# Four dense tiles instead of two in a graph-attention kernel, with the list work moved earlier

## The chip, the cores and the metric

The kernel runs on one core of one Trainium2 chip. The core has five engines with a queue each, worked off in order: PE (matrix products), DVE (vector work), ACT (activations and copies), POOL (here almost only the issue of indirect DMAs, that is gathers and scatters by a list of row numbers) and SP (the issue of plain DMAs). They meet at semaphores only. The metric is the device time of one execution in microseconds (us); less is better.

## The reference

Two layers on a graph of 4096 nodes with 128 features each. `adj` is a 4096 x 4096 matrix of 0 and 1 with about 66 ones in a row.

```python
# layer 0: attention with 8 heads over the neighbours, then a projection and a layer norm
Wh = einsum('nd,hde->hne', nodes, W); f1 = Wh . a1; f2 = Wh . a2
e = leaky_relu(f1[:, :, None] + f2[:, None, :], 0.2)
att = softmax(where(adj > 0, e, -9e15), axis=-1)
h = elu(einsum('hnm,hmd->hnd', att, Wh))
x = layernorm(nodes + elu(cat(h) @ W1 + b1)) * gamma + beta
# layer 1: of a node's neighbours every skip-th is dropped; then quantiles over the rest
svals = sort(where(keep[:, :, None], x[None, :, :], big), axis=1)   # feature by feature
agg = mean of svals at ceil(0.25 n), ceil(0.5 n), ceil(0.75 n)
out = (0.5 * agg + 0.5 * x) @ W.T + b + x
```

Both layers need, for each node, the list of its neighbours.

## The kernel before

A **tile** is 128 nodes. There are 32 tiles in six **blocks** (`BLOCKS`: 2, then five times 6); inside a block the nodes are sorted by their number of neighbours. The first layer (`gat`, from L936) runs as one long program in which four kinds of work are interleaved; the second (`sparse`, from L2180) follows it.

**The front** (`Front`, from L315) makes the neighbour lists from `adj`, in *pieces* (`pieces`, L866). For a tile: `scan` packs the row's bits into words with matmuls, `first` draws the largest words off with `max`. For a block: `second` in four parts, `place`, which scatters the block's lists to a DRAM table `rows_d` by indirect DMAs on POOL (L651), and `keep`, which stores them once more for the second layer. After the last block, `close` sets the order for the second layer. There are 69 pieces that count; 57 are left when the main loop starts.

**The list tiles** take two **half tiles** each (64 nodes; the loop index `u`). `load(u)` gathers the neighbours' features by indirect DMAs on POOL, one DMA for each slot of 128 rows (L1141), some 34 in a half tile, into a ring of six buffers, which is three half tiles. `probabilities(u)` forms the softmax of them on DVE and ACT (e at L1226), `rows_sum(u)` spreads it over columns (DVE, L1274) and sums with matmuls (PE, L1282); `collect` copies the sums, and after four half tiles `combine` takes two tiles through W, elu, W1, the layer norm (DVE up to L1367) and two scatters to `x1_d` on POOL (L1370). The loop over `u` (from L1616) emits in each turn: rows_sum(u), some pieces of the front (`advance`), probabilities(u + 1), a step of the dense tiles, load(u + 3), collect and a step of each running `combine`, and more steps of the dense tiles.

**The dense tiles** (`full`, from L1382) are the last `FULLS = 2` tiles, with the most neighbours. Their attention is made from whole rows of `adj`, without gathers of neighbours. A **unit** is one head over half a row: SP loads two 128x1024 pieces of f2 (L1457), DVE adds the mask and takes the maximum (L1468), ACT adds f1 (L1489), DVE makes the leaky relu (L1491), ACT the exponential (L1497), PE transposes 16 blocks (L1511) that ACT copies (L1516), and PE sums against x (L1523). 32 units in all. `full` is a generator: two steps to set up, one a unit, six for its `combine`. For a new tile the four quarters of the mask are fetched from `adj` by indirect DMAs on POOL (L1439) into one buffer, and turned into bf16 by DVE (L1447); the next quarter is fetched after that. x is held for this in the buffer `soon`, which is used for gathers of the second layer later.

The steps are taken when the front is done (`todo` empty): one after probabilities, one after `combine`, and one more in every second half tile, 2.5 a half tile.

**The hand-over**: near the end of the loop the dense steps are run out, and 24 gathers for the second layer's first tile (into `soon`, L1668) are issued on POOL after the last gather of the lists; then follow the last scatters to `x1_d` and the second layer, which sorts rows on DVE (L2254) with copies on ACT (L2247), its rows gathered by POOL (L2209).

A scheduler sets the final order of instructions on each engine from what is emitted; waits are semaphores.

Of the kernel before, what the change touches and what calls it, by code (L numbers as in the profile page):

```python
# [38 lines left out]
F32 = mybir.dt.float32  # L39
# [11 lines left out]
P = 128  # L51
N = 4096
D = 128
NT = N // P
H = 8
# [19 lines left out]
MERGE = 128  # L75
# [6 lines left out]
XF = D + 2 * H  # L82
# [20 lines left out]
BLOCKS = (2, 6, 6, 6, 6, 6)  # L103
# [3 lines left out]
DONE = START[-1] * P  # L107
SHARED = (("rowdata", ROW, I32), ("work", MERGE, F32), ("mask_s", C1, I32), ("k3", C3, F32))

FULLS = 2  # L110
LISTED = NT - FULLS
ROWS = 18
SPREAD = 9
TWO = 2
# [821 lines left out]
def gat(  # L936
# [28 lines left out]
    with ExitStack() as ctx:  # L965
# [131 lines left out]
        def own_row(t):  # L1097
            indices(t)
            if t % TWO == 0:
                if t < LISTED:  # L1100
                    me = tp.tile([P, TWO, XF], F32, name="me", bufs=5)
                else:
                    me = front.one.tile([P, max(BLOCKS), MERGE], F32, name="ids_a")
                    me = me.rearrange("p t c -> p (t c)")[:, : TWO * XF]
                    me = me.rearrange("p (j d) -> p j d", d=XF)
# [196 lines left out]
        def combine(t, zT, pair):  # L1302
# [66 lines left out]
            for j in range(TWO):  # L1369
                done = nc.gpsimd.indirect_dma_start(  # L1370
                    out=x1_d,
                    out_offset=bass.IndirectOffsetOnAxis(ap=index[t + j][3][:, 0:1], axis=0),
                    in_=s[:, j, :],
                    in_offset=None,
                )
                for other in stored:
                    tc.declare_no_dep(done.ins, other, reason="each node has a row of its own")
                for other in ahead:
                    tc.declare_no_dep(done.ins, other, reason="rows of earlier blocks alone")
                stored.append(done.ins)  # L1380

        def full():  # L1382

# [37 lines left out]
            ]  # L1421
            buffers = nzs + [a_is[:2]]
            units = [(j, h, q) for j in range(FULLS) for h in range(H) for q in range(2)]
            own_row(LISTED)
            own_row(LISTED + 1)
            rows = tp.tile([P, FULLS, 4], I32, name="rows_f", bufs=1)
            for j in range(FULLS):
                for q in range(4):
# [32 lines left out]
            def best(n):  # L1461
# [5 lines left out]
                for i, v in enumerate(buffers[n % 3]):  # L1467
# [10 lines left out]
                f1 = mes[LISTED + j][:, j, D + H + h : D + H + h + 1]  # L1478
# [52 lines left out]
            def close(j, h):  # L1531
# [19 lines left out]
                def turn():  # L1551
                    ps = fr.psum_w.tile([P, 2, NG1], F32, name="ps_words")
                    ps = ps.rearrange("p m c -> p (m c)")[:, :P]
                    nc.tensor.transpose(ps, z[:, :P], c["idf"])
                    nc.scalar.copy(zT[h][:, ts(j, P)], ps)

                return turn

# [8 lines left out]
            best(0)  # L1567
            exps(0)
            yield
            turn, many = None, len(units)  # L1570
            for n in range(many):
                if n + 2 < many:
                    begin(n + 2)
                changing = n + 1 < many and units[n + 1][0] != units[n][0]
                if n + 2 < many and units[n + 2][0] != units[n][0] and not changing:
                    fetch_mask(1, 0, a_is[2])
                if changing:
                    for q in range(4):
                        make_mask(q, a_is[2])
                        if q < 3:  # L1580
                            fetch_mask(1, q + 1, a_is[2])
                if n + 1 < many:
                    best(n + 1)
                pTs = [turned(n, 0), turned(n, 1)]
                if turn is not None:
                    turn()
                    turn = None
                summed(n, 0, pTs[0])
                pTs.append(turned(n, 2))
                summed(n, 1, pTs[1])  # L1590
# [4 lines left out]
                    exps(n + 1)  # L1595
                if units[n][2] == 1:
                    turn = close(*units[n][:2])
                yield
            turn()
            for _ in combine(  # L1600
                LISTED,
                zT.__getitem__,
                lambda h: [(zT[h + i].unsqueeze(1), i, i + 1) for i in range(TWO)],
            ):
                yield

        stored, ahead = [], []
        held = {u: load(u) for u in range(3)}
        advance(EARLY)
        f1s = {0: spread_f1(0)}  # L1610
# [5 lines left out]
        for u in range(halves_of):  # L1616
# [5 lines left out]
            with tc.issue_after(spread):  # L1622
                if u < 2 * START[1]:
                    advance((4, 2, 1, 1)[u])
                elif todo:
                    advance(2 if u in (5, 8) or u > 12 and u % 3 == 0 else 1)
            if u == 1:
                with tc.issue_after(front.scattered):
                    held[3] = load(3)
# [23 lines left out]
            with ExitStack() as after:  # L1653
# [1187 lines left out]
```

## Time and profile before

| | us |
|---|---|
| median of three runs (7160.54 to 7166.68) | 7163.81 |
| the profiled execution's own time | 7162.36 |
| its span, first to last instruction | 7160.6 |
| first gather of the lists starts (L1141) | 84.2 |
| last gather of the lists ends | 2811.1 |
| first gather of the second layer (L2209) | 2858.6 |

Busy in the span: PE 1368.8, DVE 5647.0, ACT 2305.9, POOL 4285.1. These averages mix two stages. In the first, up to about 2860, POOL issues one gather after another and DVE is busy about half of the time; in the second DVE is busy 4190.74 us of the 4260 from 2900 to 7160.

How to read the views: a row of groups gives line, engine, operation, tiles, count, busy time, mean of one, then the idle time of the engine just before these instructions and what ended it. "issue" stands where the engine waited for nothing that the profile shows. A view of stretches gives, for each engine, busy time and number of instructions in a stretch.

### The profile page before, as it was taken

To read this page: it belongs to the slowest core of one execution; us is meant where nothing else is said; L and a number is where in the kernel's file an instruction comes from. 1 tells how busy PE (TensorE), PEld (TensorE's weight loads), DVE (VectorE), ACT (ScalarE), POOL (GpSimd) and SP (SyncE) were. 2 spreads that over 40 slices of the span, in tenths; PEclk is the share of its full clock that TensorE was granted. 3 is DMA by queue.
4 is the path that set the end of the run, shared out by engine and by line. 5 is a ranking of instruction groups with operands and counts; after the bars stand their busy time and mean duration, and the time that the engine had idled before them with its cause. 6 is when DMAs were issued, how large, how long until landed. Compare 5 with 4: busy or idle time off the path is not lost. (4 is left out here: it accounts for less than half of the span.)

```text
span 7160.6 us, 33915 instructions
## 1 busy us (share of the span) xinstructions
PE 1368.8 (19%) x7581; PEld 1097.7 (15%) x7581; DVE 5647.0 (79%) x8486; ACT 2305.9 (32%) x2777; POOL 4285.1 (60%) x4316
## 2 busy tenths in 40 slices
PE   6342443432245563000000000000000000000000
PEld 3232332322235563000000000000000000000000
DVE  6553553544554553899999999999999999999998
ACT  3010111100023342344444434444344344444343
POOL 5777777777777777754656656446355345554500
PEclk6666666666667786555555555555555555555555
DMA  7432433332243332211111111111011111111100
GB/s 236 94 111 58 109 79 88 94 62 63 56 126 106 100 97 54 52 35 33 42 33 36 36 32 44 31 33 43 25 39 41 26 30 38 36 33 29 39 0 2
DMA packets 286970, 415.39 MB, mean 58 GB/s; under 512 B 188611, under 2 KB 189764, under 8 KB 286740
## 3 DMA queue, kind: packets, MB, share of 16 engines
q0 software_dynamic: 140560, 302.48, 17.2%
q1 hardware_dynamic: 146196, 110.66, 5.5%
q14 instruction: 153, 1.25, 0.1%
q8 instruction: 61, 1.00, 0.1%
HBM read 400.05 MB, written 13.17 MB: 58 GB/s over the span
## 5 line engine op out<-in xcount | busy, mean ns | idle before, releaser
L2254 DVE TENSOR_TENSOR rows<-low,rows 128x1024 f32<-128x1024 f32 (+7 forms) x2118 | 3425.8, 1664 | 66.7 <-ACT low L2247 43.0
L2209 POOL DMA_INDIRECT rows<-x_d,info x2054 | 2068.7, 1007 | 1704.5 <-ACT picked L2309 1087.2
L1141 POOL DMA_INDIRECT nb<-xf_d,ids x2035 | 2004.5, 985 | 639.3 <-issue 593.2
L2247 ACT COPY low<-rows 128x1024 f32<-128x1024 f32 (+8 forms) x1059 | 1452.1, 1377 | 2060.8 <-DVE rows L2254 1986.7
L2316 PE MATMUL low<-sixth_i,picked 128*128 128x128 f32 x300 | 72.6, 423 | 3960.8 <-ACT low L2247 3756.2
L1226 DVE TENSOR_TENSOR e<-nb,ps_small 128x64 f32<-128x64 f32 (+9 forms) x185 | 44.2, 241 | 875.8 <-DMA nb<-xf_d,ids 867.4
L2316 PEld LDWEIGHTS low<-sixth_i,picked 128*128 128x128 f32 x300 | 63.7, 316 | 3969.8 <-ACT low L2247 3764.9
L1282 PE MATMUL ps_z<-spread,nb 128*128 128x128 f32 x4180 | 532.1, 293 | 183.4 <-DVE spread L1274 183.3
L1282 PEld LDWEIGHTS ps_z<-spread,nb 128*128 128x128 f32 x4180 | 529.7, 210 | 200.9 <-DVE spread L1274 128.4
L2254 DVE TENSOR_TENSOR rows<-low_s,rows 128x512 f32<-128x512 f32 (+3 forms) x1056 | 531.3, 538 | 2.7 <-ACT low_s L2247 1.9
L1256 ACT ACTIVATE ps_e<-ps_e 128x288 f32<-128x288 f32 (+9 forms) x60 | 23.3, 388 | 1468.1 <-DVE ps_e L1250 1468.1
L1274 DVE TENSOR_TENSOR spread<-e,ps_small 128x1024 f32<-128x1024 f32 (+4 forms) x284 | 313.9, 1129 | 125.0 <-PE ps_z L1282 113.5
L2247 ACT COPY low_s<-rows 128x512 f32<-128x512 f32 (+3 forms) x528 | 247.6, 503 | 307.9 <-DVE rows L2254 230.3
L2356 POOL DMA_INDIRECT out<-o,info x32 | 35.0, 1094 | 383.5 <-ACT o L2352 353.1
L400 PE MATMUL ps_words<-nz,pows 128*128 128x256 bf16 (+1 forms) x544 | 239.7, 612 | 21.1 <-ACT nz L393 11.9
L393 ACT ACTIVATE nz<-a_i 128x1024 bf16<-128x1024 int32 x128 | 134.8, 1055 | 278.1 <-PE ps_words L400 184.4
L1313 PE MATMUL ps_h<-zT,w_ga 128*128 128x256 f32 x240 | 100.9, 579 | 380.0 <-DVE s L1864 328.8
L1523 PE MATMUL ps_small<-soon,lists 128*128 128x128 f32 x768 | 125.9, 322 | 166.9 <-DVE e L1235 66.3
L197 DVE SCALAR_TENSOR_TENSOR key<-key,k 128x256 f32<-128x256 f32 x320 | 148.2, 478 | 1.1
L2258 DVE TENSOR_TENSOR rows<-rows 128x256 f32<-128x256 f32 (+7 forms) x259 | 146.1, 570 | 0.0
L193 DVE MAX8 k<-key 128x8 f32<-128x256 f32 x352 | 141.5, 418 | 1.0
L1523 PEld LDWEIGHTS ps_small<-soon,lists 128*128 128x128 f32 x768 | 115.2, 232 | 174.3 <-DVE e L1235 67.2
(388 smaller groups left out, 2750.5 us busy)
## 6 DMA issues: line engine op xcount, KB each, us to landing
a_i<-in_adj SPq DMA_DIRECT2D x128, 512.0 KB
rows<-x_d,info POOLq DMA_INDIRECT x2054
nb<-xf_d,ids POOLq DMA_INDIRECT x2035
nz<-f_d SPq DMA_DIRECT2D x44, 512.0 KB
a_i<-f_d SPq DMA_DIRECT2D x20, 512.0 KB
xf_d<-xf POOLq DMA_DIRECT2D x4, 576.0 KB
soon<-xf_d SPq DMA_DIRECT2D x32, 72.0 KB
me<-rows_d SPq DMA_DIRECT2D x30, 72.0 KB
```

The source lines that it names most:

```text
L193: nc.vector.max(out=top, in_=work)
L197: nc.vector.scalar_tensor_tensor(work, work, top[:, 7:8], work, op0=ALU.is_lt, op1=ALU.mult)
L400: nc.tensor.matmul(ps_w[:, :m, ts(i, 2 * part)], self.pows[:, b, :], bits[:, :m, :, b], start=b == 0, stop=b == WBITS - 1,)
L1141: gather = nc.gpsimd.indirect_dma_start(out=rows[:, used + i, :], out_offset=None, in_=xf_d, in_offset=bass.IndirectOffsetOnAxis(ap=ids[:, ...
L1274: last = nc.vector.tensor_tensor(spread[:, :m], e[:, at : at + m, :].unsqueeze(2).to_broadcast(shape), own.unsqueeze(1).unsqueeze(3).to_br ...
L1282: product = nc.tensor.matmul(ps_z[:, g, :], rows[:, k, :D], spread[:, i].rearrange("p j h -> p (j h)"), start=i0 + i == 0, stop=i0 + i == ...
L1523: nc.tensor.matmul(fr.small[:, ts(q, P)], pT[:, ts(i, P)], xs[:, m, :] if m < NT * 3 // 4 else later[:, m - NT * 3 // 4, :], start=4 * g + ...
L2209: return nc.gpsimd.indirect_dma_start(out=row, out_offset=None, in_=x1_d, in_offset=bass.IndirectOffsetOnAxis(ap=info[:, col : col + 1], a ...
L2247: nc.scalar.copy(packed, lows)
L2254: done = nc.vector.tensor_tensor(to, packed, highs, op=op)
L2258: nc.vector.tensor_tensor(lows, lows, highs, op=ALU.min)
L2316: product = nc.tensor.matmul(made["ps"], v, to, start=i == 0, stop=i == len(found))
```

## The change

`FULLS` goes from 2 to 4, so there are 28 list tiles (56 half tiles) and four dense ones (64 units). The own rows of the dense tiles share one buffer, the mask is fetched for each next tile, and the dense tiles are combined in two pairs: the first pair's `combine` runs beside the third tile's units. The front gives two pieces a half tile from `u = 8` on (before: one, and two in every third after `u = 12`), so it ends at `u = 29` instead of 41. The dense steps are one more a half tile: 3.5 in the mean. `combine` of the list tiles takes two steps a turn in the last block. The dense steps are run out, and the 24 gathers for the second layer emitted, one half tile nearer to the end; these gathers are declared free of the dense tiles' scatters.

```diff
-FULLS = 2
+FULLS = 4
...
+                    at = t - LISTED
+                    if not at:
+                        me = front.one.tile([P, max(BLOCKS), MERGE], F32, name="ids_a")
+                        me = me.rearrange("p t c -> p (t c)")[:, : FULLS * XF]
+                        mes["full"] = me.rearrange("p (j d) -> p j d", d=XF)
+                    me = mes["full"][:, at : at + TWO, :]
...
+                if t >= LISTED:
+                    last.append(done.ins)
...
-            own_row(LISTED)
-            own_row(LISTED + 1)
+            for j in range(FULLS):
+                own_row(LISTED + j)
...
-                    nc.scalar.copy(zT[h][:, ts(j, P)], ps)
+                    nc.scalar.copy(zT[h][:, ts(j % TWO, P)], ps)
...
+            def finished(j):
+                return combine(
+                    LISTED + j,
+                    zT.__getitem__,
+                    lambda h: [(zT[h + i].unsqueeze(1), i, i + 1) for i in range(TWO)],
+                )
...
-                    fetch_mask(1, 0, a_is[2])
+                    fetch_mask(units[n + 2][0], 0, a_is[2])
...
-                            fetch_mask(1, q + 1, a_is[2])
+                            fetch_mask(units[n + 1][0], q + 1, a_is[2])
...
+                if n and n % (2 * H * TWO) == 0:
+                    steps = finished(n // (2 * H) - TWO)
+                    next(steps)
...
+                if steps is not None:
+                    next(steps, None)
                 yield
...
-                    advance(2 if u in (5, 8) or u > 12 and u % 3 == 0 else 1)
+                    advance(2 if u in (5, 8) or u > 7 else 1)
...
-                for stages in going:
+                for stages in going * (2 if u >= 2 * START[-1] else 1):
                     next(stages, None)
-            if rest is not None:
+            for _ in range(2 if rest is not None else 0):
                 next(rest, None)
-            if u + 3 == halves_of:
+            if u + 2 == halves_of:
                 for _ in rest:
                     pass
...
+                        for other in last:
+                            tc.declare_no_dep(
+                                done.ins, other, reason="rows of earlier blocks alone"
+                            )
```

More of the change, by code (lines that the diff above doesn't have):

```diff
@@ L1102, in own_row @@
                 else:
-                    me = front.one.tile([P, max(BLOCKS), MERGE], F32, name="ids_a")
-                    me = me.rearrange("p t c -> p (t c)")[:, : TWO * XF]
-                    me = me.rearrange("p (j d) -> p j d", d=XF)
+                    at = t - LISTED
[4 more added lines that the diff above has]
+                    me = mes["full"][:, at : at + TWO, :]
                 for j in range(TWO):
@@ L1477, in best @@
                     )
-                f1 = mes[LISTED + j][:, j, D + H + h : D + H + h + 1]
+                f1 = mes[LISTED + j][:, j % TWO, D + H + h : D + H + h + 1]
                 most, less = k[:, 4 * q + 2 : 4 * q + 3], k[:, 8 + q : 9 + q]
@@ L1569, in full @@
             yield
-            turn, many = None, len(units)
+            turn, many, steps = None, len(units), None
+            def finished(j):
[4 more added lines that the diff above has]
+                )
             for n in range(many):
@@ L1597, in full @@
                     turn = close(*units[n][:2])
+                if steps is not None:
+                    next(steps, None)
                 yield
             turn()
[L1600 to L1604, printed above, removed]
+            for _ in finished(FULLS - TWO):
                 yield
-        stored, ahead = [], []
+        stored, ahead, last = [], [], []
         held = {u: load(u) for u in range(3)}
```

## The prediction

> **What bounds the kernel now.** I read first the page's slices: POOL is at 7 tenths in slices 1 to 16 with DVE below it in all but the last, then DVE at 9. So there are two stages, and the change touches the first alone. The built order of the second stage's instructions is the same on all engines, so I take its 4302 us (2858.6 to 7160.6) as fixed and ask when its first gather can start.
>
> What bounds the first stage: the costliest group, and POOL's waits up to the last gather (us in total, times, longest).
>
> ```profile
> L1141 POOL DMA_INDIRECT nb<-xf_d,ids x2035 | 2004.5, 985 | 639.3 <-issue 593.2 <-PE ps_z L1282 14.0 <-DMA nb<-xf_d,ids 11.0
> ```
>
> ```profile
> POOL nb L1141 <- issue: 593.2, 1947, 0.3
> POOL nb L1141 <- PE ps_z L1282: 14.0, 8, 7.3
> POOL nb L1141 <- DMA nb<-xf_d,ids: 11.0, 36, 0.3
> ...
> POOL a_i L1439 <- DVE high L1447: 4.4, 1, 4.4
> ```
>
> The reader is to see that 2004.5 + 593.2 us of the 2727 between first and last gather are issue, each gather behind the last. A busy share of 76% is thus a full queue. Who consumes has slack; DVE's waits from 2080 to 2340 and 2380 to 2700, where the dense units run:
>
> ```profile
> DVE e L1226 <- DMA nb<-xf_d,ids: 77.5, 9, 21.9
> ```
>
> ```profile
> DVE e L1226 <- DMA nb<-xf_d,ids: 96.0, 9, 20.0
> ```
>
> DVE sits waiting for gathers 173.5 of these 580 us. The pace of POOL, in three stretches (gathers alone; lists with front, lists with units, lists alone):
>
> ```profile
> 1200.00:2000.00 800.00, 590.71 (x604) 0.63 0.32 73
> 2050.00:2720.00 670.00, 488.10 (x476) 0.78 0.38 105
> 2720.00:2812.00 92.00, 67.24 (x71) 0.65 0.25 57
> ```
>
> A gather takes 0.978, 1.025 and 0.947 us, plus 0.30 of issue. Last, POOL's timeline where a dense tile changes and at the hand-over:
>
> ```profile
> 2354.16 0.94 POOL L1439 DMA_INDIRECT a_i<-in_adj,rows_f  x1 [0.30 <-issue]
> 2359.48 1.68 POOL L1439 DMA_INDIRECT a_i<-in_adj,rows_f  x1 [4.38 <-DVE high L1447]
> 2365.47 1.74 POOL L1439 DMA_INDIRECT a_i<-in_adj,rows_f  x1 [4.31 <-DVE head_f L1484]
> 2374.53 1.29 POOL L1141 DMA_INDIRECT nb<-xf_d,ids  x1 [7.31 <-PE ps_z L1282]
> ...
> 2811.44 0.99 POOL L1370 DMA_INDIRECT x_d<-s,info  x1 [0.30 <-issue]
> 2817.45 0.95 POOL L1370 DMA_INDIRECT x_d<-s,info  x1 [3.74 <-DVE s L1367]
> 2821.18 0.98 POOL L1668 DMA_INDIRECT soon<-x_d,info  x1 [1.52 <-DMA x_d<-s,info]
> 2858.57 0.98 POOL L2209 DMA_INDIRECT xs<-x_d,info  x1 [2.04 <-ACT rows L2391]
> ```
>
> A change of dense tile makes POOL wait 4.4 + 4.3 us for masks, then 7.3 us for the ring. After the last gather POOL needs 47.5 us to the second stage, 30 of them the 24 gathers into `soon`.
>
> **The change part by part.** All in POOL's time up to the last list gather (2811.1 before).
>
> 1. *Gathers.* The built order has 1901 list gathers instead of 2035: -134. Eight more mask fetches (16 for 8). Two more scatters to `x1_d` stand before the last gather (6 behind it instead of 8). Net -124 instructions at 0.947 + 0.30 = 1.25 us: **-155 us**.
>
> 2. *Slower gathers beside dense units.* (1.025 - 0.947) x 476 = 37 us for 32 units, 1.2 us a unit. 32 more: **+37**. Bounds: 0, if the excess belongs to the stretch and not to the units, and 60, if a denser mix doubles the overlap for the new ones. I take the row.
>
> The Trainium skill ("SBUF — State Buffer", section "Who interferes with whom") says that a DVE instruction with two SBUF inputs and a GpSimd instruction that reads SBUF exclude each other for a whole instruction. Both L1468 and L1491 read two SBUF tiles, two of each a unit at 1.22 us. If each blocked POOL in full, a unit would cost 4.9 us and the 32 new ones 156, which would eat the gain. The rows show a quarter of that, and the sum goes by the rows.
>
> 3. *Masks.* Three changes of tile instead of one. In POOL's built order a quarter's fetch directly follows the one whose mask it waits for four times (two before): 2 x 4.35 = **+9**. Bounds 0 (DVE late, masks made meanwhile) and +20 (each of six).
>
> 4. *The ring.* POOL is blocked when DVE and PE lag by more than some two half tiles (ring: three). Does DVE keep up with 3.5 units a half tile? In the 580 us above it did 27 units and 14 half tiles outside gather waits in 406 us; a half tile with no units costs 14 (DVE is busy 30.9 of the 100 us from 2700, 2.2 half tiles), so a unit costs (406 - 196)/27 = 7.8 us, small waits included. After: 64 x 7.8 = 499, 21 half tiles x 14 = 294, the first dense pair's `combine` 16, three changes of tile. Before, the change stalled DVE 49 us, as the second quarter's fetch stood behind gathers; in the new order 28 to 34 gathers (35 to 42 us) stand between second and third quarter, of which DVE covers some 15 and then waits 5 for the last: about 30 each, 90. Sum some 900 us. POOL's time for the same half tiles: 695 gathers, 16 fetches, 14 scatters at 1.25 = 906, + 74 (64 x 1.16) + 17 = about 1000. DVE is at 90%: it keeps up in the mean, but has little to work off a lag. Before: 7.3 us of ring wait for one change. After I take 15: **+8**. Bounds: -7 (no wait) and +75 (lag of all three changes, 90, adds up).
>
> 5. *The front, two pieces a half tile.* A `first` costs DVE 11 x 0.42 (L193) + 10 x 0.48 (L197) + 0.8 = 10.2 us; about 0.7 more pieces a half tile are 7 us. From 400 to 2000 DVE waits 542.7 of 1600 us for gathers, 14 us in each half tile of some 43: covered. SP's loads and POOL's scatters of lists move forward with the pieces; block 3's `place` comes nine turns before its fetch instead of four. An 85 us DVE stall of before (L1161 on `me`, queued on SP behind that fetch) should vanish, worth nothing since POOL ran on. **0**; bounds -5 and +25 (a scatter whose `place` is late stops POOL; before, 3.4 us in all).
>
> 6. *PE, ACT, SP for 32 more units.* From 2050 to 2720 PE is busy 382.5 of 670, ACT 260.9; a unit is some 7 us on either, one every 15.6 us instead of 21. SP issues 64 more 512 KB loads, 34 GB/s beside 105 in that stretch; slice 0 moved 236. Covered by POOL's queue; if that cover goes, DVE waits, which is 4. **0**.
>
> 7. *The hand-over.* Now two scatter pairs of block 4 stand between last gather and `soon`; the second is of tiles 24 and 25, whose last `combine` steps come after probabilities of the last half tile. From the last gather before: DVE is done with e at +8; the new order puts four spreads (1.35 each, a wait of 4 for PE) and two elu (0.7 each) ahead: +19; layer norm 5.4 to 8.5: +26; two scatters and landing 4: +30; `soon` 30: +60; last scatters and landing 5: +65, against 47.5: **+17**. Bounds 0 and 25.
>
> Sum -155 + 37 + 9 + 8 + 17 = -84. From the profiled execution's 7162.4: 7078. The median of before is 1.4 above that execution, so this is 1.2% under it. About 0.2% (14 us) is what a measurement can tell from no change.
>
> **The rivals.**
>
> A, *DVE becomes the bound of the dense stretch.* For it: 90% of POOL's time, stalls three times. Against: 30% idle before. With the ring wait at +75 instead of +8: 7145. 10%.
>
> B, *the dense units' chain is too slow for the pace, and the kernel is slower.* Place: half tiles 30 to 50, the same three f2 buffers for more units. A unit's serial chain is load, L1468, L1489, L1491, L1497, transposes and copies; if a unit costs DVE 12.5 us instead of 7.8, stalls included, the need is 800 + 294 + 106 = 1200, POOL is held 200 less the ring's 85 cover: 115, minus the 15 counted: 7178. It decides from 12.2 us a unit on, which cancels the 84. Against: 7.8 us measured; the units' own f2 waits (L1468) are 18 us in all. 9%.
>
> C, *the front stops POOL* at scatters: +25 and its lag in later half tiles as much again: 7125. 8%.
>
> D, *gain kept*: no growth of gather time, no ring wait, short tail: -155 + 9 + 6 = 7022. 10%.
>
> **How the numbers follow.** The forecast has 63%, with its own range 7045 to 7115 (gather excess 15 to 60, ring to +30). The range of 8 in 10 takes in C and D's edge and most of A: 7025 to 7145. Below 7149.5 (faster): forecast, C, D, most of A, 0.88. B reaches 7178 and over, and A's tail lies between: slower 0.08, same 0.04.
>
> **What would show it.** L1141 x1901, its "issue" still nearly all of its idle time, last list gather near 2710, first L2209 gather near 2775; gathers in the dense stretch at 1.02 to 1.05 us; the ring wait (PE ps_z) under 40 us in all. I am wrong in 4 if that wait is over 60, in 5 if POOL waits at L651, in 7 if the hand-over takes under 50 us, in 2 if the gathers keep 0.97.

## The result and the profile after

The changed kernel takes 7175.51 us in the median of 16 runs (7162.0 to 7179.7), the kernel before 7160.3 (7157.19 to 7166.68). The ratio is 1.0019, 95% interval 1.0012 to 1.0027: slower by 15 us. The forecast was 7078 us with a range of 7025 to 7145; the result lies above the range, on the other side of no change. In four of the six sets of experiments further down, every kernel, the one before too, took 7950 to 8061 us, so a time there is compared with the kernel before in the same set only.

The profiled execution of the changed kernel took 7171.24 us itself, with a span of 7169.4, which is 8.8 us above that of before. The costliest group and POOL's waits up to the second layer (us in total, times, longest):

```profile
L1144 POOL DMA_INDIRECT nb<-xf_d,ids x1901 | 1919.1, 1010 | 693.7 <-issue 550.7
```

```profile
POOL nb L1144 <- issue: 550.7, 1807, 0.3
POOL nb L1144 <- PE ps_z L1285: 104.7, 11, 21.4
...
POOL x_d L1373 <- DVE s L1370: 15.4, 2, 15.1
...
POOL a_i L1444 <- DVE base L1452: 13.0, 3, 4.4
```

134 list gathers are gone, as the change says. But "issue" is no longer the whole of the idle time: POOL waited 104.7 us for PE to free a buffer of the gather ring (14.0 before). POOL's timeline shows where; these are six of the eleven, two of them with the mask fetches (L1444) that they follow:

```profile
735.74 0.94 POOL L1144 DMA_INDIRECT nb<-xf_d,ids  x1 [20.21 <-PE ps_z L1285]
```

```profile
772.98 0.94 POOL L1144 DMA_INDIRECT nb<-xf_d,ids  x1 [12.04 <-PE ps_z L1285]
```

```profile
1636.72 1.61 POOL L1144 DMA_INDIRECT nb<-xf_d,ids  x1 [21.38 <-PE ps_z L1285]
```

```profile
1867.12 0.94 POOL L1444 DMA_INDIRECT a_i<-in_adj,rows_f  x1 [0.30 <-issue]
1872.40 1.91 POOL L1444 DMA_INDIRECT a_i<-in_adj,rows_f  x1 [4.34 <-DVE base L1452]
1878.63 1.90 POOL L1444 DMA_INDIRECT a_i<-in_adj,rows_f  x1 [4.32 <-DVE k L1452]
1889.74 2.00 POOL L1144 DMA_INDIRECT nb<-xf_d,ids  x1 [9.21 <-PE ps_z L1285]
```

```profile
2011.86 0.94 POOL L1144 DMA_INDIRECT nb<-xf_d,ids  x1 [11.06 <-PE ps_z L1285]
```

```profile
2373.02 1.90 POOL L1444 DMA_INDIRECT a_i<-in_adj,rows_f  x1 [4.36 <-DVE base L1452]
2389.98 0.94 POOL L1144 DMA_INDIRECT nb<-xf_d,ids  x1 [15.06 <-PE ps_z L1285]
```

So the ring blocks in three places: in the front (near 736 and 773 us), where the dense tiles are set up (1637), and at and after the changes of the dense tile. Who is late there is seen in DVE's waits from 1650 to 2500 us:

```profile
DVE base L1452 <- DMA a_i<-in_adj,rows_f: 78.8, 3, 30.9
DVE nz L1473 <- DMA nz<-f_d: 75.6, 23, 43.6
DVE e L1229 <- DMA nb<-xf_d,ids: 65.8, 7, 15.5
DVE high L1452 <- DMA a_i<-in_adj,rows_f: 51.7, 2, 38.8
```

DVE waits 130.5 us for masks and only 65.8 for gathers (173.5 in the 580 us looked at before). The stretches of POOL (busy, number of gathers): front and lists, units and lists, lists alone.

```profile
1000.00:1500.00 500.00, 368.20 (x369) 0.63 0.35 84
1650.00:2500.00 850.00, 583.53 (x545) 0.84 0.44 125
2600.00:2800.00 200.00, 147.39 (x157) 0.68 0.25 56
```

A gather takes 0.998, 1.071 and 0.939 us. The hand-over, in POOL's timeline:

```profile
2803.60 0.94 POOL L1144 DMA_INDIRECT nb<-xf_d,ids  x1 [0.31 <-issue]
2804.85 0.99 POOL L1373 DMA_INDIRECT x_d<-s,info  x1 [0.30 <-issue]
2806.15 0.97 POOL L1373 DMA_INDIRECT x_d<-s,info  x1 [0.30 <-issue]
2822.23 0.96 POOL L1373 DMA_INDIRECT x_d<-s,info  x1 [15.11 <-DVE s L1370]
```

```profile
2860.49 0.98 POOL L2227 DMA_INDIRECT xs<-x_d,info  x1 [2.05 <-ACT low L2265]
```

The last list gather ends at 2804.5 us instead of 2811.1, the second layer's first gather starts at 2860.5 instead of 2858.6.

The sum, made from POOL's rows of both traces between the first and the last list gather (gather time above 0.945 us and gaps above 0.303 us are each added up):

| us | before | after | difference |
|---|---|---|---|
| indirect DMAs: 2099, 1975, at 1.248 | 2619.6 | 2464.8 | -154.8 |
| gather time above 0.945 | 84.5 | 128.9 | +44.4 |
| gaps above 0.303 | 23.1 | 126.4 | +103.3 |
| hand-over, last list gather to first L2227 | 47.4 | 55.9 | +8.5 |
| second layer to the end | 4302.0 | 4308.9 | +6.9 |

With 0.5 us from the start this is the 8.8 us of the spans. The gain of 155 us is there in full; gaps took 103 of it back and slower gathers 44.

### The profile page after: what moved, and what is told of

Read it like the earlier page. It is cut to its first block, busy times and chain, and to the rows that moved or that the text cites. A ratio compares the mean times of both kernels' runs of the same rounds, so it can differ in the third digit from the quotient of the medians.

```text
span 7169.4 us, 37194 instructions
## 1 busy us (share of the span) xinstructions
PE 1496.0 (21%) x8851; PEld 1220.1 (17%) x8851; DVE 5793.3 (81%) x8817; ACT 2517.1 (35%) x3129; POOL 4219.5 (59%) x4190
## 5 line engine op out<-in xcount | busy, mean ns | idle before, releaser
L2227 POOL DMA_INDIRECT rows<-x_d,info x2054 | 2078.8, 1012 | 1696.1 <-ACT picked L2327 1078.3
L1144 POOL DMA_INDIRECT nb<-xf_d,ids x1901 | 1919.1, 1010 | 693.7 <-issue 550.7
L1285 PE MATMUL ps_z<-spread,nb 128*128 128x128 f32 x3902 | 490.8, 291 | 219.4 <-DVE spread L1277 219.4
L1285 PEld LDWEIGHTS ps_z<-spread,nb 128*128 128x128 f32 x3902 | 486.7, 207 | 234.8 <-issue 141.7
L1259 ACT ACTIVATE ps_e<-ps_e 128x256 f32<-128x256 f32 (+9 forms) x56 | 21.8, 389 | 1108.9 <-DVE ps_e L1253 1108.9
L1277 DVE TENSOR_TENSOR spread<-e,ps_small 128x1024 f32<-128x1024 f32 (+4 forms) x268 | 292.5, 1118 | 86.7 <-PE ps_z L1285 82.9
L1528 PE MATMUL ps_small<-soon,lists 128*128 128x128 f32 x1536 | 223.0, 296 | 109.4 <-ACT lists L1521 37.6
L400 PE MATMUL ps_words<-nz,pows 128*128 128x256 bf16 (+1 forms) x544 | 239.2, 612 | 30.8 <-ACT nz L393 15.6
L1528 PEld LDWEIGHTS ps_small<-soon,lists 128*128 128x128 f32 x1536 | 205.0, 208 | 121.5 <-ACT lists L1521 47.0
L1521 ACT COPY lists<-ps_words 128x512 f32<-128x512 f32 x256 | 143.2, 584 | 70.8 <-PE ps_words L1516 39.2
L1494 ACT ACTIVATE nz<-nz,ids_a 128x1024 f32<-128x1024 f32 x86 | 98.3, 1153 | 171.5 <-DVE head_f L1473 171.1
```

Source lines behind the costliest of these rows:

```text
L400: nc.tensor.matmul(ps_w[:, :m, ts(i, 2 * part)], self.pows[:, b, :], bits[:, :m, :, b], start=b == 0, stop=b == WBITS - 1,)
L1144: gather = nc.gpsimd.indirect_dma_start(out=rows[:, used + i, :], out_offset=None, in_=xf_d, in_offset=bass.IndirectOffsetOnAxis(ap=ids[:, ...
L1277: last = nc.vector.tensor_tensor(spread[:, :m], e[:, at : at + m, :].unsqueeze(2).to_broadcast(shape), own.unsqueeze(1).unsqueeze(3).to_br ...
L1285: product = nc.tensor.matmul(ps_z[:, g, :], rows[:, k, :D], spread[:, i].rearrange("p j h -> p (j h)"), start=i0 + i == 0, stop=i0 + i == ...
L1521: nc.scalar.copy(pT, ps)
L1528: nc.tensor.matmul(fr.small[:, ts(q, P)], pT[:, ts(i, P)], xs[:, m, :] if m < NT * 3 // 4 else later[:, m - NT * 3 // 4, :], start=4 * g + ...
```

## The experiments

The theories. *Ring*: DVE stands at waits for data that queue behind POOL's own gathers, so its lag uses up the gather ring and POOL stops. *Work*: DVE simply has too much to do at the new pace. *Contention*: the slower gathers are the loss and the waits its by-product. First four kernels, run together.

**e1: the front's pace alone.**

```diff
--- before
-                    advance(2 if u in (5, 8) or u > 12 and u % 3 == 0 else 1)
+                    advance(2 if u in (5, 8) or u > 7 else 1)
```

> The kernel before with the front's new pace alone (two pieces a half tile from the eighth on; two dense tiles, two steps a half tile as before). The theory that the time is lost in the gather ring says that the 32 us of ring wait that the changed kernel shows at 736 and 773 us come from this pace and stay in the time: 7175 to 7195 us, with ring waits (PE ps_z) of 40 to 50 us in all and two of them near 740 and 775 us. The forecast's own step (the pace is covered) says 7155 to 7165 us, ring waits as before, 14 us. The theory that gathers slowed by dense work eat the gain says the same as the forecast here: no change.

Measured: 7223.48 us, ratio 1.0089 (1.0072 to 1.0106). The pace alone costs 63 us, more than either number expected. POOL's waits:

```profile
POOL nb L1141 <- issue: 583.3, 1914, 0.3
POOL nb L1141 <- PE ps_z L1282: 64.8, 10, 23.1
```

The ring waits are those of the changed kernel: 20.2 at 736, 12.2 at 773, and 23.1 at 1639, the set-up of the dense tiles, which follows the front's end. So this is not the work of four dense tiles. Against this kernel, the four dense tiles with their 3.5 steps win 48 us.

**e2: no change of mask.**

```diff
--- after
-                changing = n + 1 < many and units[n + 1][0] != units[n][0]
-                if n + 2 < many and units[n + 2][0] != units[n][0] and not changing:
+                changing = False
+                if n + 2 < many and units[n + 2][0] < units[n][0]:
```

> The changed kernel without the mask fetches and mask builds at the three changes of dense tile: the later dense tiles use the mask of the first, so their output is another. The theory that the mask changes stall VectorE and through it the ring says: the ring waits after 1850 us (51 us) fall under 15, the 12 fetches (15 us) and their own waits (17 us) go, in all 75 us: about 7100 us. If instead VectorE simply has too much work in the dense stretch, the ring waits stay and only fetches and their waits go: about 7143 us. If slowed gathers are the whole loss, also about 7143 us, with the duration of a gather in that stretch unchanged at 1.05 us or more.

Measured: 7104.87 us, ratio 0.9921 (0.9905 to 0.9938), 71 us under the changed kernel (75 expected). The gaps of POOL after 1850 us fall from 73 us to 10, those before stay (34 and 22). Gather time above 0.945 us is 137 us, so contention is not what the masks cost.

**e3: dense steps emitted later.**

```diff
--- after
             if rest is None and not todo:
-                rest = full()
+                idle += 1
+                if idle == 2:
+                    fetch(LISTED)
+                if idle == 4:
+                    rest = full()
```

> The changed kernel with the dense units started three half tiles later, the lists of the last block being loaded two half tiles ahead of them. The ring theory says: the 60 us wait of VectorE for info at 1510 to 1572 us goes, and with it the ring wait of 21 us at 1637: about 7154 us. If that wait only shows a lag that the dense units make anyway, another ring wait appears behind it and the time stays at 7170 to 7180 us.

Measured: 7178.89 us, ratio 1.0023 (1.0012 to 1.0033): no gain, as the second number expected has it. But the theory of the early wait is not tested by it: the wait for `info` is there again, 60.82 us, and so is the ring wait at 1640 (20.6). DVE's order had hardly moved: the scheduler puts the `rows_f` instructions among those of the front's last piece, as early as it may, whatever turn of the loop emits them. In the changed kernel the row is this one:

```profile
1572.05 0.15 DVE L1434 TENSOR_SCALAR rows_f<-info 128x1 int32<-128x1 int32 x1 [60.53 <-DMA info<-rows_d]
```

`info` is loaded by SP after the last block's scatters, and these stand on POOL behind the gathers of half tile 31 (1552 us; the positions they carry were ready at 1477).

**e4: three dense steps a half tile.**

```diff
--- after
-            if rest is not None and half:
-                next(rest, None)
```

> The changed kernel with three dense steps a half tile instead of three and a half. If VectorE has too much work for the pace (units of some 10 us instead of 7.8), the ring waits after 1650 us go down by half and the time to about 7150 us. If the waits come from the three mask changes and from the start, each costs what it did: 7170 to 7180 us, ring waits of 95 us or more. If slowed gathers are the loss, the same 64 units slow the same gathers: 7170 to 7180 us too.

Measured: 7198.06 us, ratio 1.0053 (1.0036 to 1.0070). Less work in each half tile made it slower by 23 us, more than any theory expected; ring waits are 120.4 us. That speaks against *work*: the three changes of mask cost at least what they did, and the units now reach to 2712 us (2524), next to the hand-over. The largest wait at the last change (20.5 us at 2535) falls on half tile 49, where the ring is shorter, as told below; no run tests that.

The four together with the later e9c, with POOL's gaps over 2.5 us in us, by place:

| | DMAs | front, 730-790 | set-up, 1640 | later | gather excess | hand-over | median |
|---|---|---|---|---|---|---|---|
| before | 2099 | 4.8 | 0 | 16.0 | 84.5 | 47.4 | 7160.3 |
| after | 1975 | 32.2 | 21.4 | 73.1 | 128.9 | 55.9 | 7175.5 |
| e1 pace alone | 2101 | 32.4 | 23.1 | 21.5 | 87.6 | 46.4 | 7223.5 |
| e2 no masks | 1963 | 34.2 | 22.0 | 10.4 | 137.2 | 55.9 | 7104.9 |
| e3 later | 1973 | 34.2 | 20.6 | 87.7 | 123.0 | 55.5 | 7178.9 |
| e4 three steps | 1973 | 34.3 | 20.3 | 93.4 | 130.8 | 58.6 | 7198.1 |
| e9c | 1973 | 33.8 | 0 | 31.4 | 131.0 | 65.6 | 7121.2 |

**e5, e8, e9, e10: which early instruction, and an order of units that needs fewer waits.** `mine` (f1 of the next tile) is held behind its half tile's spread (e5); the dense steps too, with a later set-up (e8); the units run through all heads of the left half of a row before the right, and the next tile's mask is fetched one quarter every four units, each fetch four units ahead of its use (e9); and, on the changed kernel alone, the leaky relu becomes an instruction with one operand (e10).

```diff
--- e5
-            if not half and t + 1 < LISTED:
-                f1s[t + 1] = spread_f1(t + 1)
             ps_z, behind = rows_sum(u, held.pop(u), e)
             spread = behind[-1]
+            if half and t + 1 < LISTED:
+                with tc.issue_after(spread):
+                    f1s[t + 1] = spread_f1(t + 1)
--- e8: e5, and
-            if rest is not None:
-                next(rest, None)
+            if rest is not None and idle > 4:
+                with tc.issue_after(spread):
+                    next(rest, None)
...
+            idle += not todo
+            if idle == 2:
+                fetch(LISTED)
+            if idle == 3:
+                rest = full()
+                with tc.issue_after(spread):
+                    next(rest)
--- e9: e8, and
-            units = [(j, h, q) for j in range(FULLS) for h in range(H) for q in range(2)]
+            units = [(j, h, q) for j in range(FULLS) for q in range(2) for h in range(H)]
...
+                if n % 4 == 3 and n > 3:
+                    i = n // 4 - 1
+                    if i and (i + 3) // 4 < FULLS:
+                        make_mask((i - 1) % 4, a_is[2])
+                    if i // 4 + 1 < FULLS:
+                        fetch_mask(i // 4 + 1, i % 4, a_is[2])
--- e10: after, and
-                    nc.vector.scalar_tensor_tensor(v, v, 0.2, v, op0=ALU.mult, op1=ALU.max)
+                    nc.vector.tensor_scalar(v, v, 0.2, None, op0=ALU.mult)
```

> The changed kernel with one edit: the f1 of the next tile (mine on VectorE, which waits for that tile's own row, and so for the lists of its block) is made one half tile later and held behind that half tile's spread in VectorE's order. In the changed kernel mine of tile 8 stands two half tiles ahead of its use and VectorE waits 56 us for it at 650 to 706 us. If that wait is what fills the ring at 736 and 773 us, both ring waits (32 us) go: about 7143 us. If it is the exponentials that wait behind the front's adjacency loads on ScalarE (den, 19 us at 727), a ring wait of 10 to 20 us stays there: 7155 to 7165 us. If a stall of VectorE costs nothing because the gathers are the limit elsewhere: 7170 to 7180 us.

> As the last, and the dense steps too are held behind the spread of their half tile on VectorE, the last block's lists are loaded one half tile before the dense tiles are set up, and the first dense step that needs a mask comes two half tiles after the set-up. The run that only emitted the steps later showed the same 60 us wait for info at the same place, since VectorE's order hardly moved. The theory that VectorE's fixed order puts instructions ahead of data that still stand in POOL's queue says: the wait for info and the ring wait of 21 us near 1637 go as well as the 32 us of the front; the mask changes stay: about 7122 us. The rival that VectorE has too much work in the dense stretch says that the later start packs it and new ring waits of 20 us or more come after 1900 us: 7140 us or more.

> As the last, and the dense tiles' units are in another order: all heads of the left half of a row, then all heads of the right half, the left half's sums waiting in the buffer of the transposed result. So two quarters of the mask are free for eight units, and the next tile's quarters are fetched one every four units, each fetch four units (about 1.1 half tiles) ahead of the build that waits for it. All is computed as in the changed kernel. The theory that the mask changes stall the ring since three fetches stand behind gathers within one half tile says: ring waits after 1850 us fall from 51 us to under 15 and POOL's waits for masks (17 us) go: about 7065 us, 7050 to 7085. If VectorE's work is what holds the ring, the waits stay: 7110 us or more.

> The changed kernel with the leaky relu of the dense units, which reads two operands from SBUF, replaced by a multiplication by 0.2 that reads one: the relu of the dense tiles is left out, so their output is another. If VectorE instructions with two SBUF operands are what slows the gathers beside dense units, half of these instructions go, and the sum of gather time over 0.945 us falls from 129 us to 100 to 110; the time falls by that and by ring waits that shorter VectorE work saves: 7130 to 7150 us. If the transfers of the units (512 KB loads) slow them, that sum stays at 125 to 135 us and the time falls by ring waits alone: 7150 to 7170 us.

The kernel before took 7961.97 us in this set. e5: 7985.98, ratio 1.0023 (1.0007 to 1.0038). e8: 7975.17, 1.0021 (1.0008 to 1.0034). e9: 7972.48, 1.0006 (0.9984 to 1.0029). e10: 7980.06, 1.0027 (1.0013 to 1.0042). These settle nothing. POOL of e5 waited 540.4 us for the ring here: the gathers were not the limit, so neither their number nor a wait of DVE could decide. PE's rows in the repeat of e5, between 814 and 819 us, show what was:

```profile
814.63 0.27 PE L1285 MATMUL ps_z<-spread,nb 128*128 128x128 f32 x1 [1.16 <-issue]
816.06 0.27 PE L1285 MATMUL ps_z<-spread,nb 128*128 128x128 f32 x1 [1.16 <-issue]
818.16 0.27 PE L1285 MATMUL ps_z<-spread,nb 128*128 128x128 f32 x1 [1.83 <-issue]
```

One matmul of 0.27 us every 1.4 to 2.1 us, and nothing in the profile that PE waits for.

**The same again, and the pace of the front with instructions held back** (e11: the kernel before with the pace of e1, and what e8 holds back and sets up later).

> The kernel of e5_f1 again (the changed kernel with mine of the next tile held behind its half tile), since that run fell on a chip on which the kernel before too takes 7962 us. Where the kernel before takes about 7160 us: if the wait for mine fills the ring at 736 and 773 us, about 7143 us; if the exponentials behind the adjacency loads do, 7155 to 7165 us; if neither matters, 7170 to 7180 us.

> The kernel of e8_start again (dense steps held behind their half tile, later set-up). Where the kernel before takes about 7160 us: 7122 us if VectorE's early instructions are the cause of both front and start waits; 7140 us or more if VectorE has too much work for a later start.

> The kernel of e9_order again (left halves of all heads, then right halves; one mask quarter every four units). Where the kernel before takes about 7160 us: 7050 to 7085 us if the mask changes held the ring; 7110 us or more if VectorE's work does.

> The kernel before with the front's new pace (as e1_front, which took 7223 us), and mine and the dense steps held behind their half tiles and the set-up delayed as in e8; two dense tiles. If the pace costs only through instructions that stand too early in VectorE's order, the ring waits at 738, 775 and 1640 us go (55 us) and the one change of mask stays (13 us and what follows, some 20 us in e1_front): 7160 to 7175 us. If the denser front is itself too much work for VectorE, ring waits of 20 us or more stay before 1600 us: 7185 us or more.

Again a set of that kind, the kernel before at 8044.03 us, on the very chip where e1 to e4 had run with 7160.63. e5b: ratio 0.9992 (0.9975 to 1.0010). e8b: 0.9968 (0.9952 to 0.9984). e9b: 0.9969 (0.9946 to 0.9991). e11: 1.0017 (1.0004 to 1.0029). Whether holding instructions back saves the 63 us of the pace is not told by this.

**e9c: e9 where the kernel before takes 7162.31 us.**

> The kernel of e9_order once more (left halves of all heads, then right halves; one mask quarter every four units; mine and dense steps held behind their half tiles). Its two earlier runs fell on chips on which the kernel before takes 7962 and 8044 us and engines wait for their instructions; this run asks what it does where the kernel before takes about 7160 us: 7050 to 7085 us if early instructions and mask changes held the ring; 7110 us or more if VectorE's work does.

Measured: 7121.17 us, ratio 0.9941 (0.9925 to 0.9958): 41 us faster than the kernel before, and 54 under the changed one's 7175.5 us of another set; nothing is left out. It lies in the second range expected, 7110 us or more, which was that of *work*. But DVE was not short of time: after 1500 us it still waited 182 us for gathers. And the ring waits after 1850 us did not stay: they fell from 51 to 26 us, though not under the 15 that the first range went with. So neither theory has it whole. The table above says where the time went: the ring wait at the set-up is gone (21 us), the gaps after 1850 us fall from 73 to 31 us, POOL's waits for masks from 17 us to 0.3, and the hand-over grew by 10. What did not go are the 34 us of the front, although `mine` no longer stands early. In their place the trace of e9c shows another chain, here one row each from DVE, ACT, SP and POOL:

```profile
729.89 0.46 DVE L1216 TENSOR_REDUCE den<-ps_e 128x32 f32<-128x288 f32 x1 [75.43 <-ACT ps_e L1261]
```

```profile
720.17 1.06 ACT L393 ACTIVATE nz<-a_i 128x1024 bf16<-128x1024 int32 x1 [84.83 <-DMA a_i<-in_adj]
```

```profile
696.31 0.38 SPq L1059 DMA_DIRECT2D ids<-rows_d  x1
```

```profile
687.50 0.99 POOL L651 DMA_INDIRECT rows_d<-soon,pos_i  x1 [0.30 <-DMA nb<-xf_d,ids]
```

Read upwards: block 2's lists are scattered by POOL at 687 us, behind gathers; SP stands at the load of these lists until 696; the adjacency rows (`a_i`) stand on SP behind it (from 714 us); ACT stands 84.8 us at the instruction that makes the signs of such a row; and the exponential that DVE needs for its half tile stands on ACT behind that. In the changed kernel the same queue of SP held both `me` (a tile's own row, from which `mine` is made) and `a_i`:

```profile
705.75 0.22 DVE L1164 TENSOR_TENSOR mine<-me,group 128x64 f32<-128x64 f32 x1 [55.72 <-DMA me<-rows_d]
```

```profile
717.58 1.06 ACT L393 ACTIVATE nz<-a_i 128x1024 bf16<-128x1024 int32 x1 [80.71 <-DMA a_i<-in_adj]
```

Before the change SP stood at that load until 712 us as well, but the next adjacency rows were not due until 785, and from 300 to 1500 us ACT never waited over 2.3 us for one. So e5's theory, that `mine` fills the ring, fell: taking it out of the way left the ring waits as they were. That DVE had too much work there does not fit the first of the two waits: in the changed kernel it was busy 8.8 of the 85 us from 650 to 735. Between the two waits it was busy 28.3 of 38 us, so for the second this stays open.

**e14: adjacency loads on another queue; e15: the version this points to.** e14 is e9c with one word changed in `scan`. e15 adds that a half tile's gathers are held behind scatters placed in the same turn, an earlier start, and 3.75 dense steps a half tile. e8c and e10c are e8 and e10 again.

```diff
--- e14: e9, and
-                    nc.sync.dma_start(
+                    nc.scalar.dma_start(
                         out=a_i, in_=self.adj[ts(t + j, P), ts(2 * i + q, quarter)]
                     )
--- e15: e14, and
-                held[u + 3] = load(u + 3, after=spread)
+                with ExitStack() as order_:
+                    if u > 1 and front.scattered is not put:
+                        order_.enter_context(tc.issue_after(front.scattered))
+                    held[u + 3] = load(u + 3, after=spread)
```

> The kernel of e8_start once more (the changed kernel, its units in their old order, with mine and the dense steps held behind their half tiles and the set-up later), where the kernel before takes about 7160 us. e9c took 7121 us with the new order of units on top, against 7175 us of the changed kernel. If the gain is that of the mask changes, this run keeps the ring waits of some 50 us after 1850 us and the mask waits of 17 us and takes 7150 to 7175 us; if the later set-up alone did it, 7120 to 7135 us.

> The kernel of e9c with one edit in the front: the loads of the adjacency rows (a_i) are issued from ScalarE's queue, where they are turned into signs, instead of SP's. In e9c the ring waits at 738 and 778 us (34 us) are there though mine is held back, and VectorE waits 75 us for an exponential (den) before them. If that exponential stands on ScalarE behind signs whose loads stand on SP behind the lists of block 2, which wait for scatters behind gathers, both ring waits go: 7085 to 7095 us. If the denser front is itself too much work for VectorE at that place, a ring wait of 15 us or more stays: 7100 us or more; the 128 issues cost ScalarE some 60 us more of work (0.4 to 0.5 us each on SP), which could make the exponentials later by itself: up to 7125 us.

> The kernel of e10_leaky once more (the changed kernel with the dense units' leaky relu replaced by a multiplication that reads one SBUF operand, so the dense tiles' output is another), where the kernel before takes about 7160 us. If VectorE instructions with two SBUF operands slow the gathers, the sum of gather time over 0.945 us falls from 129 us to 95 to 110 us and the time to 7130 to 7150 us; if the units' loads do it, the sum stays at 125 us or more.

> The kernel of e14 with three edits: the gathers of a half tile are held behind the scatters of the block's lists placed in that turn, so the scatters go one half tile earlier; the dense units begin three steps earlier; and they take 3.75 steps a half tile, so that the last scatters wait less at the hand-over (66 us in e9c, 47 before). All is computed. If the hand-over falls to 50 us and nothing new blocks the ring: 7065 to 7080 us. If VectorE cannot keep 3.75 units a half tile (its waits for gathers, 182 us after 1500 us in e9c, say it can), ring waits of 20 us or more come after 1900 us: 7090 us or more.

The kernel before at 8045.54 us. e8c: ratio 0.9974 (0.9957 to 0.9991). e14: 0.9956 (0.9936 to 0.9977). e10c: 1.0018 (1.0003 to 1.0034). e15: 1.0005 (0.9992 to 1.0019). e14 once more, as the last run:

> The kernel of e14_actq once more (e9c with the adjacency loads of the front issued from ScalarE's queue), for a chip on which the kernel before takes about 7160 us and e9c 7121 us. If the exponentials stand behind loads that stand on SP behind the lists of block 2, the ring waits at 738 and 778 us go: 7085 to 7095 us. If the denser front itself is too much for VectorE there, a ring wait of 15 us or more stays: 7100 us or more; with ScalarE made late by 128 issues, up to 7125 us.

7951.49 us against 7967.41, ratio 0.9978 (0.9966 to 0.9990). The expectations were for the other condition and are neither met nor refuted. e14 is faster than the kernel before in both of its sets, but so is e8c, which keeps the loads on SP, and neither shows long waits of ACT for `a_i` there (at most 3.4 us from 300 to 1500 us). Whether moving the loads frees the front's 34 us where gathers are the limit stays open. So does the share of the set-up alone (e8) in the gain of e9c, but for POOL's gaps in the table.

## Why the prediction was wrong

The sum of the prediction against the account of the traces, in us:

| step | predicted | measured |
|---|---|---|
| 1 gathers | -155 | -154.8 |
| 2 slower gathers | +37 | +44.4 |
| 3 masks | +9 | +8.6 (POOL's waits for masks: 17.3 against 8.7) |
| 4 the ring | +8 | +41.9 |
| 5 the front | 0 | +48.8 (32.2 - 4.8 in the front, 21.4 at the set-up) |
| other gaps | - | +4.0 |
| 7 the hand-over | +17 | +8.5 |
| the end | - | +6.9 |

The ring waits of +90.7 us in all (104.7 - 14.0) are parted between 4 and 5 by place, as e1 shows the first two places without any more dense work.

*Step 5 failed first and most.* It was put at 0 and measured +48.8; "covered" was argued from DVE's mean slack of 14 us a half tile. e1 shows the whole price of the pace, 63 us: 27.6 in the front's gaps, 23.1 at the set-up, 5.5 in the later gaps, 3.1 in slower gathers, and small terms. How it comes about is read from the traces, and no run takes the front's part away. At block 2, DVE waited 30.3 us for `me` before (at 724 us) and 55.7 after, with 18.8 for the exponential behind it. I counted the turns between `place` and fetch for block 3 and did not ask what stands behind block 2's fetch on SP. At the old pace nothing due stood there; at the new one the adjacency rows did, and through ACT's queue the softmax of a list tile. That I had named POOL at L651 as the sign of a failure here was the wrong place to look: it waited 3.8 us there.

The 85 us stall of DVE at block 3, which "should vanish", is gone at `me`, but the same chain put another in its place, one row each from ACT and DVE:

```profile
1024.86 1.06 ACT L393 ACTIVATE nz<-a_i 128x1024 bf16<-128x1024 int32 x1 [75.08 <-DMA a_i<-in_adj]
```

```profile
1035.72 0.42 DVE L1214 TENSOR_REDUCE den<-ps_e 128x32 f32<-128x256 f32 x1 [69.64 <-ACT ps_e L1259]
```

It cost POOL nothing: from 800 to 1600 us it has no gap over 0.5 us. So the length of a stall is not its price.

*What steps 4 and 5 both had wrong is the ring.* Six buffers were taken as three half tiles. A buffer holds 18 slots, and `load` opens a new one when the next group of a half tile does not fit. By the kernel's sizes a half tile of up to 36 slots takes two buffers, but the last three of a block of six tiles (37, 39 and 44 slots; half tiles 13 to 15, 37 to 39 and so on) take three, four and four. There the ring is about one and a half half tiles. Counted by gathers, the nine ring waits over 2.5 us of the changed kernel all stand at the first gather of a new buffer. In seven of them, 67.6 of 104.1 us, the buffer waited for is of the half tile one or two back instead of three: both waits of the front (half tile 14) and those from 1889 to 2097 (half tiles 37 to 41). So are both waits of the kernel before and all six of e9c. The stall at block 3 fell where half tiles take two buffers. No run changes the ring, so what a longer one would save is not shown.

*Step 4 failed in its price, not in its need:* +8 predicted, +41.9 measured. From 1650 to 2500 us DVE spent 784 us outside gather waits, 218 of them by the 14 us a half tile of the prediction for 15.6 half tiles; with 57 units that leaves 9.9 us a unit, where rival B needed 12.2. Without the 130.5 us of mask waits and 80 of waits for f2 it is 6.2. The predicted 7.8 is 6.0 by the same count: it held 18 us of waits for f2 and, against its words, 31 us of the old change's mask wait (2309 to 2358), which began inside the window. So the work of a unit had hardly changed. Mask waits were put at 90 us and came to 130.5. The error is what they cost. I let the ring's 85 us cover a lag. But the first change falls on half tiles 37 to 39, where the ring is short, and at the third one two mask waits (38.8 and 30.9 us) came within 50 us; POOL then stood for as long as DVE needed to its next spread, 15.1 us after the fetch at 2373. e2 shows that the masks are the cause (73 to 10 us), and e4 that fewer units a half tile do not help. In e9c, with each fetch four units ahead, POOL hardly stood for masks (0.3 us); DVE's waits for them after the set-up fell to 63 us, and the longest, 33.4 us at 2103, was followed by no gap of POOL over 2.5 us for more than 300 us.

*Step 2* was right in kind and 7 us short (1.071 us a gather beside units; 1.02 to 1.05 expected). The Trainium skill ("SBUF — State Buffer", section "Who interferes with whom") speaks of a whole-instruction exclusion between DVE instructions with two SBUF inputs and GpSimd reads; the rows here show less. A least-squares fit of the 1901 gather times of the changed kernel on their overlap with DVE's work gives 0.42 us of delay for each us that L1473 overlaps and 0.36 for L1496, and 0.05 for L1277, which takes one operand from PSUM. By the fit, the two-operand instructions slow gathers by a bit over a third of the overlap. The runs that replace L1496 by a one-operand form fell in sets where gathers are not the limit; there the fit gives 0.15 to 0.20 for it, at 0.70 us instead of 1.22 an instruction, against 0.33 to 0.40 for the old form in e5 and its repeat, which points the same way and is no proof.

*Steps 1 and 3* held. *Step 7* was half as dear: the last scatter waited 15.1 us for the layer norm, no more.

*The end* was taken as fixed and is not: from the last scatter of `out` to the end of the program it is 10.7 us in the changed kernel and 4.0 before, all of it in a drain on POOL (10.0 against 3.3). All the kernels with four dense tiles in the table show 10.0 to 10.7, e1 with two shows 4.0. The cause was not tried.

The rivals: B's number (7178) came out by luck, as its mechanism did not: a unit stayed under 12.2 us. A and C had the right signs (ring waits of 75 us and more; the front holding POOL), each alone and too small; they came together.

## What to carry to other kernels

Before speeding up a side stream, write down for each of its loads what stands ahead of it and behind it on the same queue, and whose work of the main stream then waits on an in-order engine; mean slack covers work, but need not cover such waits, and a run of the pace change alone shows their price. Count what a ring of buffers holds where it holds least, as a stall of 70 us cost nothing at block 3 and one of about 75 us at block 2 stopped the gathers. A fetch that shares a queue with the main stream lands after that queue's backlog, so issue it ahead of its use; e9c does so by four units and did not end DVE's waits, so how far ahead is enough is not shown.

## What the runs showed of the hardware

In four of six sets of runs the kernel before took 11 to 12% longer. In the profiles of these sets PE and DVE often wait with no releaser that the profile can name (in e5, PE 385.4 us at L1285, put down to "issue", and DVE 300.0 us at L1277, put down to "remote"), one matmul of 0.27 us coming every 1.4 to 2.1 us. One chip showed both conditions within an hour, so it is not a property of a chip; nor does the granted clock tell them apart (0.578 in the changed kernel, 0.583 in e5). The Trainium skill ("Runtime: NRT & Kernel Launch", section "Instruction fetch mechanics") says that an engine's sequencer streams its instructions by itself, and that the cost of going from one block of them to the next is mostly hidden. If it is the supply of instructions that is slow here, it is not hidden in these rows; whether it is, no run shows. The 71 packets of queue 8, marked as instruction, took 1.08 us each in the changed kernel and 1.09 in e5, so these transfers at least were not slower. A change that shortens POOL's queue was worth little in that condition: e9c's gain of 0.6% was 0.3% and 0% there.
